# Image loads ahead of small weights, second-image statistics ahead of the last taps, and one attention step per convolution step in the last blocks

## Chip, cores and metric

The kernel runs on one core of a Trainium2 chip. The metric is the device time of one execution in microseconds (us); before the change it is 2064.95 us, the median of three runs from 2063.49 to 2067.5.

## What is computed

The input is two images of 256 channels and 56 x 56 pixels in float32. The first layer is a group norm, a 1x1 convolution to 768 channels, a 3x3 depthwise convolution, local attention in 7x7 windows (4 heads undilated, 4 heads at dilation 2), a projection and a residual:

```
x = x + _L0_conv_ref(_gn(x), w_qkv1, w_qkv2, rpb0, rpb1, w_proj)
t = _to_tokens(x)                                   # (2, 3136, 256)
t = t + _L1_attn_ref(_ln_t(t), Wq, Wk, Wv, Wm, W1, W2, g1, b1, g2, b2)
t = t + _L1_ffn_ref(_ln_t(t), Wr, br, ln_g, ln_b, W1, b1, W2, b2)
x = _from_tokens(t, x)
# in _gn:          (v - mean) / sqrt(var + eps), 32 groups of 8 channels
# in _L0_conv_ref: y = einsum(w_qkv1, x); y = depthwise 3x3 (y); 7x7 local attention; w_proj
# in _L1_attn_ref: Q, K = elu + 1; KV = sum K v; msg = Q KV Z; norm; two-layer feed-forward; norm
# in _L1_ffn_ref:  top 2 of 8 experts, 256 -> 1024 -> 256 with gelu
```

The second layer is linear attention with a feed-forward part, and a mixture of 8 experts with two experts per token.

## The kernel before

A planner of the programming framework puts the instructions of each engine into a queue. It works from the order in which the program emits them and from its own estimate of when inputs are ready; the program's order is the priority, and an instruction that is ready sooner may be put ahead of one that was emitted earlier. The kernel steers it with three means. `tc.issue_after(ins)` puts an instruction behind `ins` in the same engine's queue. `tc.high_priority()` raises the instructions inside it. `tc.manual_schedule` in `layer1` fixes TensorE's order to the order of emission. Once the queues are made, each engine takes its own in order.

**`front`** does layer 0 and the keys of the first half of layer 1's tokens. Its parts are generators, and the order in which they are advanced is the order of emission.

- `load_x(b)` (L399) loads one image into `x_sb`, in two halves of rows and two tiles of channels, each 784 KB: channel tile 0 from SP's queue, channel tile 1 from ACT's queue. For image 0 it is called at L412, after the loads of `g8` (the group-mean matrix) and `w2` (the depthwise weights, 27 KB in runs of 36 bytes) in ACT's queue (L407, L409). In the profile `x_sb` is named `t_a`, because the memory is used for tokens later.
- `norm_image` (L473) is the group norm. VectorE takes 14 `bn_stats` (L482) and two `bn_aggr` (L485); a matmul with `g8` (L488), a few VectorE operations and a second matmul (L494) give mean and variance of each group; POOL takes the power -0.5 (L143); VectorE then normalises `x_sb` in four pieces (L500). It yields twice inside the statistics and once after the power.
- `convolutions` (L505) goes over 2 images x 6 blocks `oc` of 128 output channels x 2 halves `hf` of the rows. POOL makes nine diagonal weight matrices per block (`diag`, L514, two blocks of buffers). For each half TensorE does the 1x1 convolution (L525, 16 matmuls), ScalarE copies it into a padded tile (L531), TensorE does the 3x3 taps of the first eight rows with the diagonals (L546, 18 matmuls), and VectorE the taps of the other 20 rows (L559, eight `scalar_tensor_tensor` after a first one on ScalarE, L557). SP stores the half to `yd` in memory (L566). In the last half of image 0, `(oc, hf) == (5, 1)`, it also issues `load_x(1)`, and the generator `behind = norm_image()` is advanced after taps 3, 5, 7 and after the store. In that half of image 1, ACT loads the tokens of the first half.
- `attend(b)` is the local attention of one image: `band0` and `band1` yield once per chunk of keys. A chunk (L580 on) is score matmuls (L589, 32 rows of the array per head), a bias and mask added by VectorE (L593), an exponential on ScalarE (L598), and the product with the values (L602, 32 columns per head). After each strip come accumulation (L609), a normalisation (L619 to L629) and the projection (L358, L363), stored to `td`. A band starts only when enough blocks of the convolution have been stored.
- The loop at L860 draws one step of `convolutions`, and then `advance(PACE[b])`: up to two steps of the attention, for either image. There are eight convolution steps in a block. When the convolutions end, `cv.close()` gives up their buffers, `tokens.open()` takes the memory for the keys, and 13 steps of `first_keys` alternate with `advance(3)`. `advance(10**6)` emits what is left of the attention.

**`layer1`** starts with `merged(0, ...)` (L1519 on), which folds the key sums of the first half into a matrix `mw`: transposes `kxt`, a product with `w_v` into PSUM (`kvt`, L1542), the head mask `m32` on VectorE (L1547), a product with `w_m` (L1551), and `centre(mw)`. Then 14 groups of tokens pass through queries, keys of the second half, messages, feed-forward and routing. After the first of these steps `prepare_feed_forward` calls `centre(fw2)` (L1478 to L1480 on VectorE). `newest[0]` is the last PSUM copy that the helper `evac` gave to VectorE.

The experts (L1380, L1398) follow until the end.

Of the kernel before, what the change touches and what calls it, by code (L numbers as in the profile page):

```python
# [14 lines left out]
ALU = mybir.AluOpType  # L15
# [4 lines left out]
P = 128  # L20
B, C, HH, WW = 2, 256, 56, 56
# [10 lines left out]
NEG = -1e30  # L32
KR = (8, 7)
KC = 14
PACE = (2, 2)

EDGE = (0, 4, 11, 18, 25, 28)
S1 = [-(-2 * WW * (EDGE[j + 1] - EDGE[j]) // 32) * 32 for j in range(5)]
# [80 lines left out]
def hybrid_kernel(ctx: ExitStack, tc: tile.TileContext, a: dict, out: bass.AP):  # L119
    nc = tc.nc  # L120
# [47 lines left out]
    newest = [None, None]  # L168
# [198 lines left out]
    def front(ph):  # L367
# [31 lines left out]
        def load_x(b):  # L399
            for hf in range(2):  # L400
                cols = slice(hf * T // 2, (hf + 1) * T // 2)
                for ct in range(2):
                    eng = nc.sync if ct == 0 else nc.scalar
                    eng.dma_start(x_sb[:, ct, cols], xv[b, :, ct, cols])

        g8 = cw.tile([P, P], F32, name="g8")
        nc.scalar.dma_start(g8, a["c_g8"])  # L407
        w2 = cw.tile([P, 6, 9], F32, name="w2")
        nc.scalar.dma_start(  # L409
            w2, a["L0_conv_w_qkv2"].rearrange("(oc p) one kh kw -> p oc (one kh kw)", p=P)  # L410
        )
        load_x(0)  # L412
        wq1 = cw.tile([P, 2, 3 * C], F32, name="wq1")
        nc.sync.dma_start(wq1, a["w_qkv1_t"].rearrange("(ct p) o -> p ct o", p=P))
        wpr = bp.tile([P, 2, C], F32, name="wpr")
# [57 lines left out]
        def norm_image():  # L473

            st = sp.tile([P, 2, NG, 6], F32, name="st")
            mv = sp.tile([P, 2, 2], F32, name="mv")
            for gs in (range(0, 3), range(3, NG)):
                for ct in range(2):  # L480
                    for g in gs:
                        nc.vector.bn_stats(st[:, ct, g, :], x_sb[:, ct, g * G : (g + 1) * G])  # L482
                yield
            for ct in range(2):
                nc.vector.bn_aggr(mv[:, ct, :], st[:, ct, :, :].rearrange("p g s -> p (g s)"))  # L485
            gps = ps_c.tile([P, 4], F32, name="gps", tag="pc")
            gm = sp.tile([P, 2], F32, name="gm")
            nc.tensor.matmul(gps[:, 0:2], g8, mv[:, :, 0], start=True, stop=True)  # L488
            nc.vector.tensor_copy(gm, gps[:, 0:2])
            dv = sp.tile([P, 2], F32, name="dv")  # L490
            nc.vector.tensor_tensor(dv, mv[:, :, 0], gm, ALU.subtract)
            nc.vector.tensor_tensor(dv, dv, dv, ALU.mult)
            nc.vector.tensor_tensor(dv, dv, mv[:, :, 1], ALU.add)
            nc.tensor.matmul(gps[:, 2:4], g8, dv, start=True, stop=True)  # L494
            grs, anchors["pow"] = rstd_of(sp, gps[:, 2:4], 1e-5, "gn")
            yield
            for hf in range(2):
                cols = slice(hf * T // 2, (hf + 1) * T // 2)
                for ct in range(2):
                    nc.vector.tensor_scalar(  # L500
                        x_sb[:, ct, cols], x_sb[:, ct, cols],
                        gm[:, ct : ct + 1], grs[:, ct : ct + 1], ALU.subtract, ALU.mult,
                    )

        def convolutions():  # L505


            for _ in norm_image():
                pass
            yield 0, 0  # L510
            for b, oc in ((b, oc) for b in range(B) for oc in range(6)):
                diag = yp.tile([P, 9, P], F32, name="diag")
                for tap in range(9):
                    nc.gpsimd.tensor_scalar(  # L514
                        diag[:, tap, :], ident, w2[:, oc, tap : tap + 1], 1.0, ALU.mult, ALU.mult
                    )
                for hf in range(2):

                    r0 = hf * HH // 2
                    ypad = ypads[hf]  # L520
                    q0 = r0 - hf
                    for g0, n in ((0, 8), (8, 8), (16, 8), (24, 5)):
                        py = ps_c.tile([P, 8, WW], F32, name="py", tag="pc")
                        for ct in range(2):
                            nc.tensor.matmul(  # L525
                                py[:, :n, :], wq1[:, ct, oc * P : (oc + 1) * P],
                                x_sb[:, ct, (q0 + g0) * WW : (q0 + g0 + n) * WW],
                                start=(ct == 0), stop=(ct == 1),
                            )
                        k0 = 1 - hf + g0  # L530
                        nc.scalar.copy(ypad[:, k0 : k0 + n, 1 : WW + 1], py[:, :n, :])  # L531
                    behind = iter(())
                    if (oc, hf) == (5, 1):

                        if b + 1 < B:
                            load_x(b + 1)
                            behind = norm_image()
                        else:
                            for n0 in range(0, NA, 4):
                                tokens.load(n0, min(4, NA - n0), nc.scalar)  # L540

                    yc = yp.tile([P, HH // 2, WW], F32, name="yc")
                    pc = ps_c.tile([P, 8, WW], F32, name="pc", tag="pc")
                    for tap in range(9):
                        dy, dx = divmod(tap, 3)
                        nc.tensor.matmul(  # L546
                            pc, diag[:, tap, :], ypad[:, dy : dy + 8, dx : dx + WW],
                            start=(tap == 0), stop=(tap == 8),
                        )
                    nc.scalar.copy(yc[:, 0:8, :], pc)  # L550
                    yield b, oc
                    for tap in range(9):
                        dy, dx = divmod(tap, 3)
                        src = ypad[:, 8 + dy : dy + HH // 2, dx : dx + WW]
                        w = w2[:, oc, tap : tap + 1]
                        if tap == 0:
                            nc.scalar.mul(yc[:, 8:, :], src, w)  # L557
                        else:
                            nc.vector.scalar_tensor_tensor(  # L559
                                yc[:, 8:, :], src, w, yc[:, 8:, :], ALU.mult, ALU.add  # L560
                            )
                        if tap in (3, 5, 7):
                            next(behind, None)
                        if tap % 3 == 2:
                            yield b, oc
                    st = nc.sync.dma_start(  # L566
                        yd[b][oc * P : (oc + 1) * P, hf * T // 2 : (hf + 1) * T // 2],
                        yc.rearrange("p h w -> p (h w)"),
                    )
                    anchors["store"] = st.ins  # L570
                    next(behind, None)
            yield B - 1, 6

        qT0 = bp.tile([P, HH, WW], F32, name="qT0")
# [56 lines left out]
        held = {}  # L631
# [215 lines left out]
        def advance(n):  # L847
            nonlocal at
            while n > 0 and at < B and need[at] <= done[at]:
                need[at] = next(atts[at], None)  # L850
                if need[at] is None:
                    at += 1
                n -= 1

        for k, (b, blocks_done) in enumerate(convolutions()):
            if k == 0:
                with tc.issue_after(anchors["pow"]):
                    bias_tables()
            done[b] = blocks_done
            if b > 0:  # L860
                done[b - 1] = 6
            advance(PACE[b])
        cv.close()
        ps_e = ph.enter_context(tc.tile_pool(name="p3pe", bufs=1, space=PSUM))
        tokens.open()
# [546 lines left out]
    def layer1(ctx, tk, behind=(None, None)):  # L1412
# [19 lines left out]
        with lin as ph:  # L1432
# [41 lines left out]
            def centre(w):  # L1474

                n = w.shape[1]
                m = sm.tile([P, 4], F32, name="wmean")
                nc.vector.tensor_reduce(m[:, :n], w, AX.X, ALU.add)  # L1478
                nc.vector.tensor_scalar(m[:, :n], m[:, :n], 1.0 / C, None, ALU.mult)
                nc.vector.tensor_tensor(w, w, m[:, :n].unsqueeze(2).to_broadcast([P, n, C]), ALU.subtract)  # L1480
# [1 line left out]
            hb = wp.tile([P, 4], F32, name="hb_sb")  # L1482

            def prepare_feed_forward():
                centre(fw2)

                hb_ps = ps_h.tile([P, 512], F32, name="hb", tag="h")
                for oc in range(4):
                    for k in range(2):
                        nc.tensor.matmul(  # L1490
                            hb_ps[:, oc : oc + 1], fw1[:, 2 + k, oc * P : (oc + 1) * P], g1b1[:, k, 1:2],
                            start=(k == 0), stop=(k == 1),
                        )
                nc.vector.tensor_copy(hb, hb_ps[:, 0:4])
                for k in range(2):
                    nc.vector.tensor_scalar(fw1[:, 2 + k, :], fw1[:, 2 + k, :], g1b1[:, k, 0:1], None, ALU.mult)
# [22 lines left out]
            def merged(b, kxs, kc):  # L1519
# [20 lines left out]
                for hg in range(2):  # L1540
                    for ct in range(2):
# [1 line left out]
                            pv[:, hg * P : (hg + 1) * P], w_v[:, ct, hg * P : (hg + 1) * P],  # L1543
                            kxt[:, ct, hg, :], start=(ct == 0), stop=(ct == 1),
                        )
                for hg in range(2):
                    nc.vector.tensor_tensor(kvt[:, hg, :], pv[:, hg * P : (hg + 1) * P], m32, ALU.mult)  # L1547
                yield
                pm = ps_a.tile([P, 512], F32, name="mwp", tag="a")
                for hg in range(2):  # L1550
# [450 lines left out]
```

## Time and profile before

| What | Value |
|---|---|
| median of 3 runs | 2064.95 us (2063.49 to 2067.5) |
| the profiled execution's own time | 2068.74 us |
| its span, first to last instruction | 2067.0 us |
| TensorE busy | 1930.8 us, 93% |
| VectorE busy | 1024.7 us, 50% |
| POOL, ScalarE busy | 670.4 us, 633.3 us |
| mean granted TensorE clock | 0.973 |
| first large matmul (L525) starts at | 27.34 us |
| image 1's first L525 starts at | 280.16 us |
| last L546 of the convolutions ends at | about 593 us |
| first keys (L275) on TensorE at | 626.67 us |
| last local-attention projection ends at | 793.5 us |
| experts from about | 1340 us to the end |

The times inside the kernel are positions in that one profiled execution, counted from its first instruction. In the lines quoted below, "PE" is TensorE, "DVE" is VectorE, "ACT" is ScalarE, "SPq" and "ACTq" are DMA issues by those engines, and `x4` is the number of instructions that a line merges. An arrow in brackets names what the engine waited for before it. In a table of windows, PEclk is the granted TensorE clock as a share of full speed.

### The profile page before, as it was taken

Reading aid. Unit: us, or ns where it says so; the run is one execution under the profiler, and the core shown is the slowest. Engines: PE = TensorE matmul, PEld = TensorE weight load, DVE = VectorE, ACT = ScalarE, POOL = GpSimd, SP = SyncE. Lnnn points to the kernel's source line nnn. Section 1 sums busy time; section 2 is a strip of 40 time slices with the busy share of each in tenths; the row PEclk is TensorE's granted clock in tenths of the full one; section 3 lists DMA queues with packets and bytes.
Section 4 is the critical chain, followed back from the end, with each engine's and each line's share of the span. In section 5 each row is a group of like instructions: output and inputs, shape, how many; then the busy total and the mean of one; then the engine's idle time right before and its main releaser. Section 6 shows DMA issues by size and latency. Waiting matters only on the chain.

```text
span 2067.0 us, 27940 instructions
## 1 busy us (share of the span) xinstructions
PE 1930.8 (93%) x10102; PEld 1353.2 (65%) x10102; DVE 1024.7 (50%) x2629; ACT 633.3 (31%) x1258; POOL 670.4 (32%) x772
## 2 busy tenths in 40 slices
PE   4999989999998888999999998999999999999996
PEld 2544444554435455566665657878888888888885
DVE  5978877775986656455555554342111211121111
ACT  1323323333333332334333333332222222222332
POOL 5621011111013333345534444543333323333221
PEclk9999989999979999999999999999999999999998
DMA  4642422335342115001111142567667676676995
GB/s 107 169 103 72 138 87 56 110 114 116 87 140 68 32 55 167 1 16 36 45 39 49 47 138 78 151 197 225 192 200 194 186 207 189 189 197 193 289 282 161
DMA packets 189785, 264.67 MB, mean 128 GB/s; under 512 B 26295, under 2 KB 149509, under 8 KB 189391
## 3 DMA queue, kind: packets, MB, share of 16 engines
q1 hardware_dynamic: 160782, 220.81, 34.9%
q0 software_dynamic: 20576, 29.75, 7.5%
q10 hardware_dynamic: 8272, 12.15, 1.8%
q8 instruction: 84, 1.38, 0.3%
q14 instruction: 71, 0.57, 0.1%
HBM read 196.38 MB, written 70.55 MB: 129 GB/s over the span
## 4 chain that ended last, share of the span: by engine, by line
PE 64%; DVE 14%; DMA 5%; POOL 4%; ACT 3%; issue 3%; SPq 1%; ACTq 0%; DVEq 0%; POOLq 0%
PE ph L1380 16%; PE py L1398 15%; PE p L1640 5%; PE po L602 4%; PE pc L546 4%; PE py L525 4%; DVE yc L559 3%; PE s_ps L589 3%; DVE p L593 2%; POOL rs L262 2%; DMA y<-yt,idi 2%; PE s_ps L363 2%; PE kp L293 2%; PE kx L306 2%; DMA xr<-xs 1%
## 5 line engine op out<-in xcount | busy, mean ns | idle before, releaser
L1380 PE MATMUL ph<-xe,w1e 128*128 128x256 f32 (+1 forms) x1696 | 362.3, 371 | 3.8 <-ACT hT L1384 2.3
L1398 PE MATMUL py<-w2e,hT 128*128 128x256 f32 x1616 | 359.0, 379 | 0.0
L1384 ACT ACTIVATE hT<-ph,sv 128x256 f32<-128x256 f32 (+1 forms) x424 | 196.4, 464 | 498.5 <-PE ph L1380 492.8
L1380 PEld LDWEIGHTS ph<-xe,w1e 128*128 128x128 f32 x1696 | 310.4, 191 | 45.7 <-ACT hT L1384 3.5
L1398 PEld LDWEIGHTS py<-w2e,hT 128*128 128x128 f32 x1616 | 302.5, 190 | 38.7
L559 DVE SCALAR_TENSOR_TENSOR yc<-ypad,w,yc 128x1120 f32<-128x1120 f32 x192 | 267.0, 1393 | 34.9 <-ACT yc L557 31.8
L160 POOL DMA_INDIRECT y<-yt,idi x101 | 161.2, 1596 | 225.6 <-DVE yt L1404 132.0
L546 PE MATMUL pc<-ypad,diag 128*128 128x448 f32 x432 | 174.4, 545 | 0.5 <-ACT ypad L531 0.5
L593 DVE TENSOR_TENSOR p<-s_ps,tab 98x340 f32<-98x340 f32 (+5 forms) x240 | 138.0, 601 | 62.4 <-PE s_ps L589 60.4
L598 ACT ACTIVATE p<-p 98x680 f32<-98x680 f32 (+5 forms) x120 | 111.8, 931 | 180.1 <-DVE p L593 175.3
L525 PE MATMUL py<-t_a,wq 128*128 128x448 f32 (+1 forms) x384 | 156.0, 536 | 9.1 <-DVE t_a L500 5.9
L1336 DVE CAST idi<-xr 128x2 int32<-128x2 f32 (+1 forms) x53 | 9.8, 185 | 305.8 <-DMA xr<-xs 301.0
L1404 DVE SCALAR_TENSOR_TENSOR yt<-py,eq,yt 128x256 f32<-128x256 f32 x101 | 48.6, 483 | 211.3 <-PE py L1398 209.7
L589 PE MATMUL s_ps<-qT,kT 32*98 32x170 f32 (+5 forms) x960 | 130.0, 410 | 20.7 <-DVE p L593 18.3
L262 POOL TENSOR_TENSOR rs<-rs,mhalf 128x2 f32<-128x2 f32 (+2 forms) x89 | 65.4, 741 | 197.0 <-DVE rs L261 155.5
L589 PEld LDWEIGHTS s_ps<-qT,kT 32*98 32x98 f32 (+1 forms) x960 | 57.2, 173 | 106.4 <-DVE p L593 61.1
L546 PEld LDWEIGHTS pc<-ypad,diag 128*128 128x128 f32 x432 | 78.1, 189 | 72.0 <-issue 68.4
L514 POOL TENSOR_SCALAR diag<-ident,w 128x128 f32<-128x128 f32 x108 | 77.6, 738 | 127.0 <-PE pc L546 118.0
L1362 POOL TENSOR_SCALAR yt<-b2e,eq 128x256 f32<-128x256 f32 x101 | 47.1, 475 | 213.1 <-DMA b2e<-in_L_ffn_b 213.0
L525 PEld LDWEIGHTS py<-t_a,wq 128*128 128x128 f32 x384 | 70.3, 196 | 70.1 <-issue 53.8
L160 POOL DMA_INDIRECT xs<-row,si x98 | 96.2, 981 | 57.8 <-DVE si L1764 30.5
L1640 PE MATMUL p<-m2T,fw 128*128 128x512 f32 (+2 forms) x224 | 93.8, 541 | 0.0
(357 smaller groups left out, 2585.5 us busy)
## 6 DMA issues: line engine op xcount, KB each, us to landing
w1e<-in_L_ffn_W SPq DMA_DIRECT2D x53, 1024.0 KB
w2e<-in_L_ffn_W SPq DMA_DIRECT2D x53, 1024.0 KB
yd<-yc SPq DMA_DIRECT2D x24, 784.0 KB
ld<-yd SPq DMA_DIRECT2D x28, 448.0 KB
xr<-xs SPq DMA_DIRECT2D x48, 260.0 KB
b2e<-in_L_ffn_b SPq DMA_DIRECT2D x53, 128.0 KB
yr<-y SPq DMA_DIRECT2D x11, 512.0 KB
td<-t_i SPq DMA_DIRECT2D x24, 224.0 KB
```

Source lines behind the costliest of these rows:

```text
L160: ins = nc.gpsimd.indirect_dma_start(out=dst[:, :], out_offset=bass.IndirectOffsetOnAxis(ap=index, axis=0), in_=src, in_offset=None, **kw,)
L262: newest[1] = nc.gpsimd.tensor_tensor(r[:, :n], r[:, :n], mhalf[:, :n], ALU.pow).ins
L525: nc.tensor.matmul(py[:, :n, :], wq1[:, ct, oc * P : (oc + 1) * P], x_sb[:, ct, (q0 + g0) * WW : (q0 + g0 + n) * WW], start=(ct == 0), sto ...
L546: nc.tensor.matmul(pc, diag[:, tap, :], ypad[:, dy : dy + 8, dx : dx + WW], start=(tap == 0), stop=(tap == 8),)
L559: nc.vector.scalar_tensor_tensor(yc[:, 8:, :], src, w, yc[:, 8:, :], ALU.mult, ALU.add)
L589: nc.tensor.matmul(s_ps[:nk, j, :n].rearrange("p (i j) -> p i j", j=nj), kT[hs], q[hs], start=True, stop=True,)
L593: nc.vector.tensor_tensor(p[:nk, 2 * pr : 2 * pr + 2, :n].rearrange("p h (i j) -> p h i j", j=nj), s_ps[:nk, :, :n].rearrange("p h (i j) - ...
L598: nc.scalar.activation(p[:nk, :, :n], p[:nk, :, :n], AF.Exp)
L1380: nc.tensor.matmul(p1, x.w1[:, ct, j * P : (j + 1) * P], x.xe[:, ct, :], start=(ct == 0), stop=(ct == 1),)
L1384: nc.scalar.activation(hT[:, j, :], p1, AF.Gelu, bias=x.sv[:, 4 + j : 5 + j])
L1398: nc.tensor.matmul(py, hT[:, j, h * P : (h + 1) * P], x.w2[:, j, :], start=(j == 0), stop=(j == NJ - 1),)
L1640: nc.tensor.matmul(p1[:, :w], fw1[:, k, oc * P : (oc + 1) * P], rhs, start=(k == 0), stop=(k == 3))
```

## The change

It has six parts.

1. `load_x(0)` stands ahead of the loads of `g8` and `w2`.
2. `norm_image` yields once after all statistics and aggregates instead of twice inside the statistics. The last aggregate is remembered as `anchors["stats"]`.
3. In the last half of image 0, the statistics of image 1 are emitted ahead of tap 4 (before: after taps 3 and 5), and tap 4 on VectorE is put behind the last aggregate. The group mean and the power follow after tap 4, and the normalisation after tap 5, both with high priority (before: after tap 7, and after the store).
4. `PACE` is 2 attention steps per convolution step while the block is below 5, and 1 from block 5 on, in both images.
5. `centre(fw2)` is put behind `newest[0]` on VectorE.
6. The two mask multiplications of `merged` get high priority.

```diff
-PACE = (2, 2)
+PACE = 2
...
+        load_x(0)
         g8 = cw.tile([P, P], F32, name="g8")
         nc.scalar.dma_start(g8, a["c_g8"])
         w2 = cw.tile([P, 6, 9], F32, name="w2")
...
-        load_x(0)
         wq1 = cw.tile([P, 2, 3 * C], F32, name="wq1")
...
             for gs in (range(0, 3), range(3, NG)):
                 for ct in range(2):
                     for g in gs:
                         nc.vector.bn_stats(st[:, ct, g, :], x_sb[:, ct, g * G : (g + 1) * G])
-                yield
             for ct in range(2):
-                nc.vector.bn_aggr(mv[:, ct, :], st[:, ct, :, :].rearrange("p g s -> p (g s)"))
+                anchors["stats"] = nc.vector.bn_aggr(
+                    mv[:, ct, :], st[:, ct, :, :].rearrange("p g s -> p (g s)")
+                ).ins
+            yield
...
+                        if tap == 4 and b + 1 < B:
+                            next(behind, None)
...
-                            nc.vector.scalar_tensor_tensor(
-                                yc[:, 8:, :], src, w, yc[:, 8:, :], ALU.mult, ALU.add
-                            )
-                        if tap in (3, 5, 7):
-                            next(behind, None)
+                            held = tap == 4 and b + 1 < B and (oc, hf) == (5, 1)
+                            with tc.issue_after(anchors["stats"]) if held else nullcontext():
+                                nc.vector.scalar_tensor_tensor(
+                                    yc[:, 8:, :], src, w, yc[:, 8:, :], ALU.mult, ALU.add
+                                )
+                        if tap in (4, 5):
+                            with tc.high_priority():
+                                next(behind, None)
...
                     anchors["store"] = st.ins
-                    next(behind, None)
...
-            advance(PACE[b])
+            advance(PACE if blocks_done < 5 else 1)
...
-                centre(fw2)
+                with tc.issue_after(newest[0]):
+                    centre(fw2)
...
-                for hg in range(2):
-                    nc.vector.tensor_tensor(kvt[:, hg, :], pv[:, hg * P : (hg + 1) * P], m32, ALU.mult)
+                with tc.high_priority():
+                    for hg in range(2):
+                        nc.vector.tensor_tensor(kvt[:, hg, :], pv[:, hg * P : (hg + 1) * P], m32, ALU.mult)
```

Counted from the generators, the convolution loop emits 131 of the 174 attention steps before the change and 122 after it: nine more are left for the time after the convolutions. Of those, 39 go with the keys in both kernels; after the last keys, 4 steps remain before and 13 after.

## The prediction

> **What bounds the kernel now.** I read the page first, then TensorE's waits stretch by stretch, then each engine's timeline around the places that the diff names, and the table of windows for the clock.
>
> ```profile
> PE 1930.8 (93%) x10102; PEld 1353.2 (65%) x10102; DVE 1024.7 (50%) x2629; ACT 633.3 (31%) x1258; POOL 670.4 (32%) x772
> PEclk9999989999979999999999999999999999999998
> ```
>
> TensorE is the bound: 93% busy, 136 us idle in all. A change of order can only win idle time, or time in which the clock was low. From 850 us on nothing in the diff differs (the experts alone are 727 us), so I look before that. The first place is the start:
>
> ```profile
> 5.84 1.68 DVE L482 BATCH_NORM_STATS2 st<-t_a 128x6 f32<-128x448 f32 x3 [4.84 <-DMA t_a<-in_x]
> 11.44 6.27 POOL L514 TENSOR_SCALAR diag<-ident,w 128x128 f32<-128x128 f32 x18 [8.95 <-DMA w<-in_L_conv_w_qkv]
> 12.93 3.78 DVE L482 BATCH_NORM_STATS2 st<-t_a 128x6 f32<-128x448 f32 x7 [5.41 <-DMA t_a<-in_x]
> 20.43 2.20 DVE L482 BATCH_NORM_STATS2 st<-t_a 128x6 f32<-128x448 f32 x4 [3.71 <-DMA t_a<-in_x]
> 25.43 0.72 POOL L143 TENSOR_TENSOR rs_gn<-rs_gn,mhalf 128x2 f32<-128x2 f32 x1 [6.94 <-DVE rs_gn L142]
> 27.34 8.15 PE L525 MATMUL py<-t_a,wq 128*128 128x448 f32 x16 [2.19 <-DVE t_a L500]
> ```
>
> The statistics wait three times for the image; the last piece is seen only at 20.43, and the first convolution starts 6.9 us later. The second place is the change of image:
>
> ```profile
> 257.31 2.72 DVE L482 BATCH_NORM_STATS2 st<-t_a 128x6 f32<-128x448 f32 x5
> 271.87 0.54 DVE L485 BATCH_NORM_AGGREGATE mv<-st 128x2 f32<-128x42 f32 x2
> 279.01 1.10 DVE L500 TENSOR_SCALAR t_a<-t_a,gm,rs_gn 128x1568 f32<-128x1568 f32 x1 [0.55 <-POOL rs_gn L143]
> 280.16 5.59 PE L525 MATMUL py<-t_a,wq 128*128 128x448 f32 x8 [3.70 <-DVE t_a L500]
> ```
>
> These statistics waited for no data: VectorE put attention and taps ahead of them. Meanwhile TensorE had attention alone. The windows (columns: length, then busy us of PE, PEld, DVE, ACT, POOL, then clock, DMA share, GB/s) show what that costs:
>
> ```profile
> 250.00:264.00 14.00, 12.39 (x107) 5.26 (x106) 13.82 (x24) 4.32 (x5) 3.99 (x10) 1.00 0.03 8
> 264.00:277.00 13.00, 12.06 (x98) 5.98 (x98) 9.84 (x21) 3.79 (x4) 0.00 (x0) 0.61 0.21 79
> 277.00:286.00 9.00, 5.84 (x10) 2.90 (x11) 7.36 (x10) 0.74 (x2) 0.73 (x1) 0.62 0.34 89
> 592.00:627.00 35.00, 30.54 (x238) 13.14 (x237) 27.58 (x70) 9.10 (x10) 9.80 (x13) 0.61 0.22 64
> 627.00:694.00 67.00, 57.38 (x446) 35.10 (x447) 47.02 (x114) 24.20 (x35) 22.38 (x27) 0.97 0.29 68
> ```
>
> Where attention runs alone (264 to 277, 592 to 627) the clock is 0.61; where convolutions or keys run with it, 0.97 to 1.00. Busy time there hides lost time. The third place is the mask of `merged`:
>
> ```profile
> 802.16 0.48 DVE L1547 TENSOR_TENSOR kvt_sb<-kvt,m 128x128 f32<-128x128 f32 x2
> 802.50 2.08 PE L1551 MATMUL mwp<-w_m,kvt_sb 128*128 128x256 f32 x4 [4.38 <-DVE kvt_sb L1547]
> ```
>
> [...] (16 L602 of one shape take 1.14 us at 258.6, 1.93 at 602.6)[...]. [...] ACT's queue had moved its last image bytes by 14.2 us, but the piece was seen at 20.43, just when SP's scattered 676-value load of the bias table (`turned`, issued 6.52) was done, 20.64. [...] Diagonals take 0.35 us alone (6.27/18) and 1.25 beside taps (22.45/18, at 66.9 us).
>
> **Part 1, image first.** Nothing is added; two ACT issues (0.40 + 0.47 us) and the 768 runs of 36 bytes of `w2` go behind the image. Image 0 is 3.21 MB; between 4 and 6 us the queues moved 421 GB/s. From 3.0 us it needs 7.6 us: 10.6. The first piece was seen about 0.9 us after its data, so the last at 11.5[...]. Eight statistics remain then: 8 x 0.54 = 4.3, end 15.8 (before: 22.6). From there to L525 was 4.7: 20.5 instead of 27.34, at best 6.8 us saved. What is late next is `w2`: its small runs start at 10.6 instead of 3.0, and took about 6.4 us by the DMA view of each us. POOL's 18 diagonals wait for it, and in POOL's queue they stood ahead of the power. I expect `w2` seen between 15.5 and[...] 21.5, and 0 to 18 diagonals (0 to 6.3 us) queued ahead of the power, whose free time is 18.7. L525 then starts between 20.5 and 29.7, that is -6.8 to +2.4. I take `w2` at 17 and nine diagonals (3.2): power 20.2, L525 22.1, **-5.2 us**. The bias tables later on POOL (to 66.8) keep their time; diagonals of block 2 follow until 78.2 and were wanted at 84.2, so 5.2 us still fit.
>
> **Parts 2 and 3, statistics of image 1.** The same 14 statistics and two aggregates (8.1 us of VectorE) move ahead of tap 4. The loads are not moved past anything: the second halves go out at 234.45 (SP) and 235.72 (ACT), right after the last L525 that reads the old image, and their data ran until about 242. Six statistics then left take 3.3: aggregate 246, not 271.87. From aggregate to L525 it took 4.8 us at the start, 8.3 here; so L525 of image 1 can come at 251 to 255, not 280. The added wait holds tap 4: behind it on VectorE are taps 5 to 8, attention adds (L593) and SP's store of the half. Before, tap 4 ran after 245 anyway, so it costs nothing if the planner's landing time is right; each us that it is early is a stalled VectorE (2.60 us at 219.1 before), starving L593. Worth is not 25 us, but what TensorE lost from 264 to 286: 22.0 - 17.9 = 4.1 idle and 13 x 0.39 + 9 x 0.38 = 8.5 of clock, 12.6. Lower end 0 (the stretch forms elsewhere), more only if the similar one at 310 to 326 (5.1 of clock) goes too. I take six tenths: **-7.5**.
>
> **Part 4, pace.** Nine steps leave the convolutions for after the last keys: about seven chunks. In 592.9 to 626.7, attention alone, ten chunks took 3.4 us each; in company one costs TensorE 2.4 (L589 1.25, L602 1.1). Seven lose 7 us; `merged` and the first queries can fill a part: +5.5, range 0 to 14 (4.4 each, as from 606 to 614.9). On the gain side the last half's taps crept from 576 to 606 with VectorE full; less attention ends them sooner and shortens the half-speed stretch before the keys (13.6 of clock + 4.5 idle): -3, range 0 to -8. Net **+2.5**.
>
> **Parts 5 and 6.** The masks could go at 798.1, when L1542 ends: L1551 3.6 us sooner. But VectorE is idle only 0.49 + 1.37 us between there and the `ks` (L245, 812.1) for which TensorE waits next, 2.53 us. So **-1.9**, range 0 to -3.6. `centre(fw2)` at 807.18 already followed the copy at 806.51; the new order costs 0. If it slipped ahead of L245 more than now, up to +2.
>
> **Sum:** -5.2 - 7.5 + 2.5 - 1.9 = -12.1. The profiled execution took 2068.74 (span 2067.0 and 1.7 around it), so 2056.6; it ran 3.8 above the median, so against the median 2064.95 - 12.1 = **2053**.
>
> **Rivals.** (a) *Power behind the diagonals*: part 1 gives nothing, the rest -6.9: 2058. For it: POOL's order before. Against: the power is emitted first. (b) *Given back*: TensorE is 93% full, and the attention-only stretch merely moves; only 2 us stay: 2063. For it: nine steps more run alone. (c) *Slower*: the tail after the last keys is attention alone at half clock, and image 1's last tokens, which wait for its projections, come late. Its price is 14 us; parts 1 to 3 pay 6 and the masks 2: 2071. It decides once the tail costs above 12. For it: 592 to 627. (d) *All of it*: 6.8 + 12.6 + 5.1 - 2.5 = 22: 2043.
>
> **Chances:** forecast 0.45 (own range 2047 to 2059), (a) 0.17, (b) 0.16, (c) 0.14, (d) 0.08. About 0.2% (4 us) is what a measurement can tell from no change. Faster: forecast, (d), most of (a), a little of (b): 0.67; same: the rest of (a), (b): 0.18; slower: 0.15. The range 2042 to 2068 leaves out (c) and a tail of (d).
>
> **What would show it.** First L525 near 22, power ahead of or among the diagonals; last L485 near 246 and image 1's L525 before 256; clock near 1.00 from 250 to 290; fewer than 35 us at 0.61 before the keys; L1551 without its wait. I am wrong if `w2` holds POOL, if VectorE idles on the second-half load, or if a low-clock stretch follows the last keys.

## The result, and the profile after

The changed kernel takes **2090.85 us** (median of 4 runs, 2087.42 to 2092.7) against 2065.72 for the kernel before (4 runs, 2063.49 to 2067.5): a ratio of 1.012, 95% interval 1.0102 to 1.0138. It is 25 us slower where 12 us faster was predicted. On a second chip the same kernel took 2086.14 against 2067.34 (1.0099, 1.0063 to 1.0136). The profiled execution took 2089.58 us, its span is 2087.8.

The page of the changed kernel, first the engines, then the row of the granted clock:

```profile
PE 1947.5 (93%) x10102; PEld 1364.5 (65%) x10102; DVE 1028.0 (49%) x2629; ACT 633.0 (30%) x1258; POOL 679.9 (33%) x772
PEclk9999999999978997999999999999999999999997
```

TensorE does the same 10102 matmuls and is busy 16.7 us longer, again at 93%. The row of the clock (slices of 52 us) now has three low slices in the first half: two from 574 to 678 us, and one from 783 to 835. The start of the changed kernel (line numbers differ from those before by up to eight: L482 is L481 here, L525 is L526, L589 is L595, L1551 is L1559):

```profile
10.97 4.32 DVE L481 BATCH_NORM_STATS2 st<-t_a 128x6 f32<-128x448 f32 x8 [0.55 <-DMA t_a<-in_x]
19.40 6.30 POOL L515 TENSOR_SCALAR diag<-ident,w 128x128 f32<-128x128 f32 x18 [16.90 <-DMA w<-in_L_conv_w_qkv]
25.64 0.85 POOL L726 MEMSET acc<- 128x896 f32 x1
26.45 0.73 POOL L143 TENSOR_TENSOR rs_gn<-rs_gn,mhalf 128x2 f32<-128x2 f32 x1
28.36 4.00 PE L526 MATMUL py<-t_a,wq 128*128 128x448 f32 x5 [10.56 <-DVE t_a L501]
```

The statistics end at 15.3 instead of 22.6 and the power's input is ready at 18.0, but the power runs at 26.45: POOL, idle for 16.90 us until `w2` is seen at 19.40, takes all 18 diagonals and a clear first, which stand ahead of the power in its queue. The first convolution is 1 us later than before. The change of image:

```profile
239.13 1.68 DVE L481 BATCH_NORM_STATS2 st<-t_a 128x6 f32<-128x448 f32 x3 [0.95 <-DMA t_a<-in_x]
254.46 0.53 DVE L483 BATCH_NORM_AGGREGATE mv<-st 128x2 f32<-128x42 f32 x2
260.36 1.86 POOL L143 TENSOR_TENSOR rs_gn<-rs_gn,mhalf 128x2 f32<-128x2 f32 x1 [1.34 <-DVE rs_gn L142]
263.41 7.96 PE L526 MATMUL py<-t_a,wq 128*128 128x448 f32 x16 [0.83 <-DVE t_a L501]
```

Image 1 starts 16.8 us sooner (263.41, not 280.16), and its last L547 comes 29.7 us sooner. The attention does not: most of its chunks are 4 to 8 us later through image 1's convolutions, and 20 us later at the end. The windows show where the clock was low (length, then busy us of PE, PEld, DVE, ACT, POOL, then clock, DMA share, GB/s):

```profile
250.00:264.00 14.00, 9.92 (x67) 4.67 (x66) 13.37 (x25) 2.42 (x3) 8.54 (x11) 0.76 0.02 5
264.00:277.00 13.00, 13.00 (x45) 6.21 (x44) 9.45 (x11) 4.08 (x6) 0.00 (x0) 0.86 0.51 154
562.00:604.70 42.70, 35.55 (x260) 17.27 (x258) 36.68 (x69) 13.22 (x19) 8.80 (x12) 0.76 0.46 133
770.00:797.00 27.00, 25.23 (x218) 13.46 (x219) 14.63 (x36) 6.98 (x10) 2.04 (x4) 0.62 0.11 33
797.00:815.00 18.00, 16.56 (x82) 10.93 (x82) 8.99 (x24) 3.22 (x7) 0.71 (x2) 0.91 0.53 151
```

The fourth row is new. After the last keys, 770 to 797, nine chunks of attention run alone at a clock of 0.62. Before, the same place (the 18 us after the last keys) was this:

```profile
628.00:776.00 148.00, 127.95 (x1007) 80.16 (x1008) 89.54 (x213) 48.06 (x70) 50.64 (x60) 0.97 0.21 53
776.00:794.00 18.00, 17.71 (x101) 12.35 (x99) 9.53 (x22) 2.29 (x5) 2.24 (x4) 1.00 0.44 120
```

Those were projections and queries at full clock. And the masks of `merged` in the changed kernel:

```profile
821.24 0.47 DVE L1555 TENSOR_TENSOR kvt_sb<-kvt,m 128x128 f32<-128x128 f32 x2
821.57 1.65 PE L1559 MATMUL mwp<-w_m,kvt_sb 128*128 128x256 f32 x3 [4.88 <-DVE kvt_sb L1555]
```

`kvt` is ready at 816.7, yet the masks come last in a row of statistics on VectorE; the wait is 4.9 us, not shorter than 4.4.

**A ledger.** From each trace I took, up to the first feed-forward matmul of layer 1 (L1640 before), TensorE's idle time and its busy time, and counted busy time at half clock as half. In both traces the granted clock is either 1.00 or 0.50 (in windows of 1 us it was 0.50 from 599 to 626 before, and from 777 to 800 in the changed kernel); half clock stands for the 0.50. In the changed kernel eight L293 took 1.99 us at 1.00 (at 639.03) and 3.78 at 0.50 (at 629.03). What is left is the work. It is the same in both kernels, 722.7 and 724.9 us; idle is 91.3 and 95.5, and time at half clock 85.3 and 105.8. So the 17.3 us that are lost up to there are 4 of idle, 10.9 of clock and 2 of work, which is as close as the method is. The runs say the same: each lists its span and mean clock, and span x (1 - clock) is the time lost to the clock. Over the 31 runs of before beside e1 it averages 56.7 us with 2007.3 left; over the 4 of the changed kernel 72.6 with 2016.1. Of the 25 us, 16 are clock; the runs don't tell idle time and work apart in the other 9.

The same by stage, for the kernels below (length in us, chunks of attention in it, us at half clock, of which half is lost; "alone" is from the last L546 to the first keys, counted as the first L293; the keys end at their last L293):

| kernel | convolutions | alone | keys | after the keys | sum |
|---|---|---|---|---|---|
| before | 592.3, 82, 34 | 35.7, 10, 27 | 148.4, 27, 10 | 76.1, 1, 14 | 852.6 |
| changed | 562.7, 76, 17 | 42.0, 8, 21 | 165.1, 27, 31 | 100.1, 9, 38 | 869.9 |
| pace alone (e1) | 566.2, 76, 34 | 39.3, 8, 17 | 160.8, 27, 21 | 99.7, 9, 38 | 866.0 |
| changed, four per key (e4) | 571.9, 76, 44 | 39.3, 8, 17 | 183.5, 36, 31 | 70.8, 0, 21 | 865.4 |
| pace, image 0 (e5) | 572.1, 76, 44 | 39.4, 8, 17 | 180.8, 35, 51 | 71.9, 1, 7 | 864.3 |
| pace, image 1 (e6) | 589.2, 82, 24 | 22.4, 6, 15 | 145.7, 23, 23 | 99.6, 9, 38 | 857.1 |
| large matmuls in the tail (e12) | 565.1, 76, 17 | 42.1, 8, 21 | 171.8, 27, 51 | 102.9, 9, 17 | 881.8 |
| attention ahead (e16) | 596.0, 82, 38 | 19.9, 4, 10 | 184.3, 33, 58 | 73.7, 1, 14 | 873.9 |
| three steps (e17) | 587.9, 82, 34 | 35.4, 10, 27 | 151.3, 28, 0 | 59.8, 0, 7 | 834.5 |

The work up to there is 721 to 728 us in all of them but e12, which adds 14. Single executions scatter: up to the keys, the changed kernel, e4 and e12 have one and the same order on TensorE, and 17, 44 and 17 us at half clock in the convolutions; up to the last keys the changed kernel and e12 have the same order too, and 31 and 51 us at half clock among the keys.

### The profile page after: what moved, and what is told of

The parts are those of the page before. It is cut to its first block, busy times and chain, and to the rows that moved or that the text cites. A ratio compares the mean times of both kernels' runs of the same rounds, so it can differ in the third digit from the quotient of the medians.

```text
span 2087.8 us, 27949 instructions
## 1 busy us (share of the span) xinstructions
PE 1947.5 (93%) x10102; PEld 1364.5 (65%) x10102; DVE 1028.0 (49%) x2629; ACT 633.0 (30%) x1258; POOL 679.9 (33%) x772
## 4 chain that ended last, share of the span: by engine, by line
PE 63%; DVE 16%; POOL 5%; DMA 4%; ACT 4%; issue 3%; SPq 0%; DVEq 0%; ACTq 0%; POOLq 0%
PE ph L1386 16%; PE py L1404 16%; PE p L1648 5%; DVE yc L565 5%; PE po L608 4%; PE py L526 4%; PE pc L547 3%; PE s_ps L595 3%; DVE p L599 2%; PE kp L293 2%; POOL rs L262 2%; DMA y<-yt,idi 2%; PE kx L306 2%; PE s_ps L363 1%; PE py L1660 1%
## 5 line engine op out<-in xcount | busy, mean ns | idle before, releaser
L547 PE MATMUL pc<-ypad,diag 128*128 128x448 f32 x432 | 173.5, 544 | 0.6 <-ACT ypad L532 0.6
L526 PE MATMUL py<-t_a,wq 128*128 128x448 f32 (+1 forms) x384 | 154.2, 532 | 14.6 <-DVE t_a L501 11.4
L595 PE MATMUL s_ps<-qT,kT 32*98 32x170 f32 (+5 forms) x960 | 138.4, 415 | 28.1 <-DVE p L599 21.2
L515 POOL TENSOR_SCALAR diag<-ident,w 128x128 f32<-128x128 f32 x108 | 84.2, 800 | 173.9 <-PE pc L547 157.0
L595 PEld LDWEIGHTS s_ps<-qT,kT 32*98 32x98 f32 (+1 forms) x960 | 60.3, 175 | 115.9 <-DVE p L599 65.8
L547 PEld LDWEIGHTS pc<-ypad,diag 128*128 128x128 f32 x432 | 78.6, 189 | 71.9 <-issue 69.5
L526 PEld LDWEIGHTS py<-t_a,wq 128*128 128x128 f32 x384 | 69.7, 195 | 76.3 <-issue 53.0
```

The lines of the kernel that those rows point to most:

```text
L526: nc.tensor.matmul(py[:, :n, :], wq1[:, ct, oc * P : (oc + 1) * P], x_sb[:, ct, (q0 + g0) * WW : (q0 + g0 + n) * WW], start=(ct == 0), sto ...
L547: nc.tensor.matmul(pc, diag[:, tap, :], ypad[:, dy : dy + 8, dx : dx + WW], start=(tap == 0), stop=(tap == 8),)
L595: nc.tensor.matmul(s_ps[:nk, j, :n].rearrange("p (i j) -> p i j", j=nj), kT[hs], q[hs], start=True, stop=True,)
```

## The experiments

My theory after the comparison was rival (c), the pace; the rival to it was that the earlier start of image 1 (parts 2 and 3) takes the convolutions away from beside the attention.

**e1, the pace alone.**

```diff
-            advance(PACE[b])
+            advance(PACE[b] if blocks_done < 5 else 1)
```

> The kernel before with one edit: one attention step per convolution step in block 5 of both images, two elsewhere. Theory (pace): the nine steps that leave the convolutions run after the last keys with nothing beside them at half clock, and the last projections and all of layer 1 come that much later; then this kernel alone is 15 to 25 us slower than before, its last chunk near 790 to 800 instead of 777, with a half-clock stretch of over 15 us after the last keys. Rival (statistics): the loss comes from image 1's earlier start, which takes convolution work away from beside the attention; then this kernel is within 4 us of before.

2083.26 us, 1.0104 (1.0086 to 1.0122): 17.7 us slower. The last keys come at 766.3 and the last chunk at 793.8 (columns as above):

```profile
766.30:793.80 27.50, 26.06 (x223) 13.78 (x225) 14.63 (x36) 6.97 (x10) 2.04 (x4) 0.60 0.12 32
```

A half-clock stretch of 23.9 us begins between them and ends at 796.0. Part 4 carries most of the loss.

**e2, the changed kernel with the old pace** (`advance(PACE)`).

> The changed kernel with two attention steps per convolution step everywhere, all other parts kept. Theory (pace): the loss of 25 us goes, and what is left are the gains of the statistics and the masks: 2050 to 2066 us. Rival (statistics): it stays 10 us or more above before, 2076 or later, since image 1's convolutions still run ahead of the attention.

2064.55, 0.9995 (0.9979 to 1.0012). The loss is gone; no gain is left. Image 1 still starts early (267.09), so its early start is not what costs: the rival falls.

**e3, the statistics alone** (the diff of parts 2 and 3 on the kernel before).

> The kernel before with the statistics of image 1 ahead of tap 4 and the raised norm steps, nothing else. Theory (pace): image 1's first convolution comes near 263 instead of 280, the low clock between 264 and 286 shrinks, and the time falls by 2 to 10 us. Rival (statistics): slower by 8 us or more.

2061.32, 0.9989 (0.9971 to 1.0007): perhaps 2 us, not told from nothing. There is no loss here either, but against the rival this run says less than e2: image 1 starts at 273.89, and counted from the first convolution of its own execution that is only some 1.5 us sooner than before.

**e4, the tail beside the keys** (`advance(4)` for `advance(3)` in the changed kernel).

> The changed kernel with four attention steps per key step instead of three, so that the 13 steps left after the last keys go beside the keys (13 key steps, 13 more steps). Theory (pace): with no attention left alone the tail from the last keys to the last projection shortens from 45 us towards 20, and the time falls by 12 us or more, to 2079 or below. Rival (statistics): the attention is late whatever it stands beside, and the time stays within 5 us of the changed kernel.

2086.18, 1.0099 (1.0063 to 1.0136). A miss: no chunk is left after the last keys and the two last stages take 254.3 us instead of 265.2, but the median fell by less than 5 us, not by 12, and beside the second measurement of the changed kernel (1.0099) by nothing. The keys' stage grew from 165 to 184 us.

**e5 and e6, the pace in one image only.**

```diff
-            advance(PACE[b])
+            advance(1 if (b, blocks_done) == (0, 5) else 2)           # e5
+            advance(1 if b == 1 and blocks_done >= 5 else 2)          # e6
```

> The kernel before with one attention step per convolution step only in block 5 of image 0. Counted from the code, the eight steps that leave there come back in block 4 of image 1, where before attention had run out of finished rows, so again four steps are left after the last keys. Theory (tail): without a tail there is no loss: 2052 to 2066 us. Rival (any thinning of attention beside convolutions costs, for TensorE is the bound): half of the 18 us of the pace change, 2072 or more.

> The kernel before with one attention step per convolution step only in block 5 of image 1: 13 steps instead of four are left after the last keys. Theory (tail): the whole loss of the pace change is here, 2080 to 2088 us, with the last chunk 20 us or more after the last keys. Rival (any thinning costs): about half of it, 2071 to 2077.

e5: 2076.57, 1.004 (1.0022 to 1.0058), 8 us slower. e6: 2083.63, 1.0082 (1.0051 to 1.0113), 15 to 17 us slower; its profiled execution was the quickest of the four. So image 1's block carries the tail and most of the loss, but the theory of the tail alone falls: e5 has no tail and loses. The trace of e5 shows why. Image 1's convolutions start 11 us earlier, the attention is 10 us later, and what lags behind runs between the first and the second key step (the columns as above):

```profile
612.00:645.00 33.00, 31.82 (x209) 14.75 (x208) 18.60 (x44) 8.45 (x10) 4.97 (x6) 0.59 0.06 18
```

TensorE is 96% busy there, with attention but for some 4 us of matmuls of the key steps, at a clock of 0.59. So attention without company costs here too, and not only after the keys. The losses of e5 and e6 together are more than the 17.7 of e1: they do not add.

**e7 and e12, is it the company?** Extra matmuls that nobody reads, ahead of each pair of score matmuls in the chunks emitted after the last keys of the changed kernel:

```diff
+                if warm[0]:                                           # e7
+                    nc.tensor.matmul(s_ps[:, 0, 320:448], ident, ident, start=True, stop=True)
...
+                if warm[0]:                                           # e12
+                    for j in range(2):
+                        nc.tensor.matmul(s_ps[:, j, 288:512], ident, wpr[:, 0, 0:224], start=True, stop=True)
```

> The changed kernel with one more matmul of 128x128 (rows it writes are read by nobody) ahead of each pair of score matmuls of the chunks emitted after the last keys: 14 matmuls, about 0.15 us each, 2 us of added work. Theory (clock): attention alone is slow because its matmuls of 32 rows or 32 columns leave the array at half clock; large matmuls mixed in end the stretch of 24 us at half clock earlier and the time falls by 4 to 12 us, to 2079 to 2087. Rival (attention alone is slow for its own waits, the clock follows): no gain, 2089 to 2094.

> The changed kernel with two matmuls of 128x128 by 224 ahead of each pair of score matmuls of the chunks emitted after the last keys (28 in all, read by nobody), a fourth to a third of TensorE's time there. One look, for the clock alone. Theory (small matmuls: the share of 32-row and 32-column work sets the clock): the half-clock stretch after the last keys, 24 us, shrinks to under 10. Rival (it is not the share of large matmuls): it stays over 17.

e7, 2 us of large matmuls among 30: 2101.8 (1.014, 1.0101 to 1.018), no help, the half-clock time after the keys even 47.8 us. e12, 14 us among 30, is one execution, of 2098.7 us; its keys, which the edit does not touch, had 20 us more at half clock than those of the changed kernel, so its time says nothing of the tail. What counts is the window from its last keys to its last chunk:

```profile
779.00:809.00 30.00, 29.79 (x271) 17.98 (x273) 14.98 (x36) 6.98 (x10) 1.11 (x2) 1.00 0.10 30
```

The half clock is gone from the window (the 17 us in the table come later, from 830 on). The nine chunks, seven of them with added work of 14 us in all, take 30.0 us; without it they take 27.5. So here the low clock of attention alone (0.60 in e1) came with its small matmuls (32 rows or 32 columns of the array), and large matmuls beside it (1.00 in e12) were nearly free. Gaps are no explanation: e12 has fewer of them (TensorE idles 0.2 us of 30, in e1 1.4 of 27.5), but in the keys of e17 below TensorE idles 10% at full clock, and in e5 above 4% at 0.59. No run added as many small matmuls instead, so that it is their size rests on this one execution and on e5 and e17.

**e8, part 1 with the power put ahead of the diagonals**, on the kernel before.

```diff
+        load_x(0)
         g8 = cw.tile([P, P], F32, name="g8")
...
+                with tc.issue_after(anchors["pow"]):
                     for tap in range(9):
```

> The kernel before with the image's loads first, and with the 9 diagonals of each block made to follow the power of the statistics on GpSimd. Theory (part 1 failed because 18 diagonals stood ahead of the power once the small weights came late): the power runs near 18.5, the first convolution starts at 19.5 to 21.5 instead of 22.5 to 27, and the time falls by 3 to 6 us, to 2059 to 2063. Rival (given back): the start moves but the first attention chunk stays at its place near 105 and the time stays within 2 us of before.

2070.11 against 2068.67, 1.0011 (0.9998 to 1.0024). The rival holds:

```profile
18.25 0.72 POOL L143 TENSOR_TENSOR rs_gn<-rs_gn,mhalf 128x2 f32<-128x2 f32 x1 [14.98 <-DVE rs_gn L142]
20.16 7.42 PE L526 MATMUL py<-t_a,wq 128*128 128x448 f32 x16 [2.19 <-DVE t_a L500]
54.10 3.39 SPq L643 DMA_DIRECT2D tab<-fp  x4
57.60 1.68 SPq L567 DMA_DIRECT2D yd<-yc  x1
65.09 1.23 ACT L558 ACTIVATE yc<-ypad,w 128x1120 f32<-128x1120 f32 x1 [12.63 <-DMA yd<-yc]
66.79 5.55 PE L526 MATMUL py<-t_a,wq 128*128 128x448 f32 x8 [6.48 <-ACT yc L551]
```

The first convolution starts at 20.16, 7 us earlier, as the sum for part 1 had it at best. But a store of a half stands in SP's queue behind loads of the bias tables (L643), which come no sooner (54.10, and 49.81 before); ScalarE waits 12.6 us for the store's buffer, and TensorE 6.5 for ScalarE. The convolution at 66.79 starts no earlier than before (66.56): the gain is gone.

**e9, e10, e11, the other parts on the changed kernel**, all on one chip; e9 is the changed kernel itself, e10 has the old order of loads, e11 the old statistics.

> The changed kernel itself, as the ground for the two beside it on this chip: slower than before by 20 to 28 us.

> The changed kernel with the order of the first loads as before (the two small loads ahead of the image). Theory (in the changed kernel the late small weights put 18 diagonals and a clear ahead of the power, so the first convolution starts at 27.5 to 29 against 22.5 to 27 with the old order): the first convolution starts 1 to 6 us earlier and the time falls by 0 to 5 us. Rival (a start that comes earlier is given back at the diagonals of block 2): no difference over 2 us.

> The changed kernel with the statistics of image 1 as before (spread over taps 3, 5, 7 and the store). Theory (the statistics bring image 1's convolutions forward but not the sum of the work, so they are worth only the low clock around the change of image, 2 to 5 us with the old pace): 0 to 6 us slower than the changed kernel. Rival (with the thinner pace the statistics add to the attention that is left over): 3 to 8 us faster.

e9 2086.14 (1.0099, 1.0063 to 1.0136), 18.8 us slower where 20 to 28 were expected; e10 2081.16 (1.0072, 1.0044 to 1.01), e11 2092.24 (1.0129, 1.0093 to 1.0164). By the medians part 1 costs 5 us and parts 2 and 3 gain 6 in this surrounding; the intervals overlap. For part 1 the start is firmer: in seven executions with the new order the first L525 starts at 27.5 to 30.6, mean 28.7; in twelve with the old, 22.5 to 27.3, mean 24.9.

**e13 and e14, what is left.** e13 is the kernel before with parts 5 and 6; e14 is the changed kernel with the old pace and the old loads.

> The kernel before with parts 5 and 6 alone (masks raised, centre of the experts' weights after the newest statistics). Theory: they move at most 2 us, 2063 to 2067 where before is at 2066, and TensorE's wait for the masks stays near 4.4 us, for in the changed kernel it was still 4.9. Rival (they are the rest of the loss that pace, loads and statistics leave open): 3 to 8 us slower.

> The changed kernel with the old pace and the old order of loads: statistics, masks and centre are what is left. Theory (parts 2 and 3 gain 4 to 6, part 1 costs 3 to 5, part 4 costs 18): 3 to 7 us faster than before, the only combination of the change's parts below before. Rival (with the old pace nothing of them is seen): within 2 us of before.

e13: 2070.04 against 2068.67, 0.9998 (0.9985 to 1.001). The wait for the masks does fall, which I had not expected, to 1.93 us, but a later start of `kx` before it (a wait of 2.54 for ScalarE instead of 1.4) takes part of it, and nothing is seen in the time. e14: 2068.44, 0.9993 (0.9973 to 1.0013). A miss of mine: with the old pace nothing of the statistics is seen either.

**e15 and e16, attention with less of it alone.** e15 adds to e14 a first key step at high priority and four attention steps per key step; e16 puts the attention steps of image 1's block 5 at high priority in the kernel before (`with tc.high_priority() if b == 1 and blocks_done >= 5 else nullcontext():` around `advance`).

> The kernel of the run beside it (old pace, old loads) with the first key step at high priority and four attention steps per key step. Theory (attention alone between the last convolution and the first keys is half speed for want of large matmuls): keys start 10 us or more earlier, the stretch at half clock of 20 to 37 us before them shrinks, and the time falls by 3 to 10 us more. Rival (the attention left over only moves behind the keys): no gain, or slower.

> The kernel before with the attention steps of image 1's block 5 at high priority, so that fewer of them are left between the last convolution and the first keys. Theory (attention alone runs at half clock for want of large matmuls): 4 to 6 chunks instead of 10 stand alone there, the half-clock time from the last convolution to the first key step falls from 27 us to under 18, and the time falls by 3 to 8 us against before. Rival (the stretch alone is only pushed behind the keys, as with earlier keys): no gain, or slower by 5 us or more.

Both miss: 2093.53 (1.011, 1.0076 to 1.0143) and 2078.37 (1.0068, 1.0041 to 1.0095). The stretch ahead of the keys did shrink, to 4 chunks in both, but the half-clock time came back among the keys, 42 and 58 us: in e16 there are 42 us between the third and the fourth key step. Here attention that was put ahead of the keys pushed them apart, and stood alone between them.

**e17 and e18, the opposite of part 4.**

```diff
-            advance(PACE[b])
+            advance(3 if b == 1 and blocks_done >= 5 else PACE[b])
```

> The kernel before with three attention steps per convolution step in block 5 of image 1, the opposite of part 4. Counted from the code only three more steps fit (finished rows run out), so one step is left after the last keys instead of four, all of them projections. Theory (what counts is chunks without company): at most three chunks move, 0 to 4 us faster. Rival (thicker attention makes VectorE the bound of the convolutions): 3 us or more slower.

> The changed kernel with the old order of loads and with three attention steps per convolution step in block 5 of image 1 instead of one (two elsewhere): statistics, masks and centre beside the opposite of part 4. Theory (the parts add: three steps gain 9 us, statistics 0 to 4): 8 to 13 us faster than before. Rival (the gain of three steps hangs on one particular order, and another start of image 1 undoes it): within 4 us of before.

e17: **2054.87** against 2064.12, 0.9954 (0.9935 to 0.9972). e18: **2054.72** against 2066.59, 0.9952 (0.9935 to 0.9969). Both beat before and after; e17 gains 9 us where 0 to 4 were expected. In e17 nothing changes up to the first keys but for a start 4 us earlier; then (keys, and the 5 us after them):

```profile
623.00:775.00 152.00, 136.45 (x1069) 86.48 (x1070) 95.70 (x225) 49.42 (x72) 51.47 (x60) 1.00 0.23 59
775.00:780.00 5.00, 5.00 (x28) 3.72 (x27) 1.81 (x3) 1.17 (x3) 1.90 (x3) 1.00 0.76 243
```

Three more steps are emitted with the convolutions, so each key step has later attention beside it and three projections less are left over. The keys run wholly at full clock with 12 us more work in them (by the ledger), and the stage after them is 16 us shorter. At the first L1640 this trace is 18 us ahead of that of before, 12 of them idle time and 7 clock; over the runs beside each other, 6 of the 9 us are clock. e18 shows that this does not hang on one order; nothing is seen of a gain of the statistics on top of it.

## Why the prediction was wrong

**What bounds the kernel** held: work is nearly constant (2 us more), and time is won or lost in idle time and clock. The windows at 0.61 were read rightly, as attention alone.

**Part 1** (-5.2). The statistics ended at 15.3 (15.8 predicted), and `w2` was seen at 19.40, inside 15.5 to 21.5. The 21.5 was an estimate from one pair of times before (the last piece of the image seen at 20.43, `turned` done at 20.64). Here ACT's queue had moved all of `w2` by 14 us, 5.4 before it was seen, and SP, which waited for `turned`, went on at 21.61; what `w2` waited for in between is not shown. I took 17 and nine diagonals ahead of the power; there were 18 and a clear, so rival (a) was the true case, at the price of about +4 against the mean start of the old order. And even the full gain is given back (e8), at a queue that the sum had not followed: SP's, where stores stand behind table loads. I had only followed the tables on POOL.

**Parts 2 and 3** (-7.5). The statistics do come sooner and image 1 starts at 263 instead of 280, but not at 251 to 255, and the aggregate came at 254.5, not 246: from 239 on, VectorE took the statistics one by one between attention and taps. Nor is the earlier start mainly theirs. Counted from the first convolution of its own execution, image 1 starts at 252.8 before, at 251.4 and 246.0 with the statistics and the old pace (e3, e14), at 241.3 with the pace alone (e1) and at 235.1 in the changed kernel: the thinner attention of part 4 brought more of it. The worth is 0 to 6 us (e3, e14, e11).

**Part 4** (+2.5) is the step that failed: its mechanism was named, its size was wrong. I priced the tail at +5.5 (seven chunks at 3.4 alone less 2.4 in company) and put -3 beside it for taps that end sooner. Measured alone, part 4 costs 17.7. The price alone was nearly right: 27.5 us for nine chunks, 3.1 each. Wrong was the saving. Seven chunks at 2.4 and 3 more should have brought the last keys 20 us forward; in e1 they came 10.2 forward, of which 4 are an earlier start. Two terms are behind this.

The 2.4 in company was too much, because it adds groups of matmuls that overlap in the trace of before:

```profile
258.59 0.58 PE L602 MATMUL po<-p,v 98*32 98x221 f32 x8
258.99 0.56 PE L602 MATMUL po<-p,ones 98*32 98x221 f32 x8
259.48 0.63 PE L589 MATMUL s_ps<-qT,kT 32*98 32x221 f32 x8
```

The first two add up to 1.14 us, but the third starts 0.89 after the first. Counted once, a chunk at full clock takes TensorE 1.9 us (mean from 100 to 592 us: 0.98 for its L589, 0.89 for its L602), and (30.0 - 14) / 9 = 1.8 in e12. So each chunk in the tail costs 1.2 to 1.3 us more than in company, not 1.0, and there are eight more of them, not seven: about 10 us. The table has it as 24 us more at half clock after the keys, of which 12 are lost; this one does not scatter, for in all six traces with this tail (the changed kernel twice, e1, e6, e10, e11) there are 37.5 us at half clock there.

The -3 did not come. The half-clock time ahead of the keys did fall, from 27 to 17, but among the keys it rose from 10 to 21 (one execution each, and the order of the changed kernel alone gave 31 and 51 there). The convolutions are 26 us shorter in e1, but 16 of these come back before the last keys. By the ledger 12 of the 16 are work, scores, transposes and projections of attention that had stood beside the convolutions, and none is clock. In all, e1's trace is 13.4 us behind that of before at the first L1640, and 11.6 of these are clock.

**Parts 5 and 6** (-1.9): 0, as far as can be told (e13). In the changed kernel the masks were raised and still came behind a dozen instructions of statistics, at 821.24.

**Rivals.** (c) named the mechanism, the place and the sign. Its price of 14 for the tail is near the 12 that the table shows lost there, and low beside all of part 4 (17.7), and the 6 and 2 us that the other parts should have paid were not there: 2071 became 2091.

**Open.** Part 4 (17.7), part 1 (about 4) and parts 2, 3 (0 to -6) make 16 to 22. The two measurements of the changed kernel are 25 and 19 us above before, so up to some 9 us of the first are not laid to a part; the clock of a single execution varies that much (over the 31 runs of before beside e1 the time lost to it was 43 to 64 us). Taking part 4 alone out of the changed kernel (e2) wins back all of it, so part 4 may cost more beside the other parts than on its own; no run here settles that.

## What to carry to other kernels

When a kernel's bound engine runs at two speeds, as TensorE did here (clock 1.00 and 0.50), draw up its ledger as work, idle and low clock; if the work is constant, ask of a reordering what it does to idle time, and which small matmuls lose the large ones beside them. Price a piece of work by what it adds to the engine's time, not by the sum of instructions that overlap. A chunk of small matmuls was cheap here beside large ones (1.8 to 1.9 us, 3.1 alone), so a thinner pace near the end of the large work left a rest that cost more later (17.7 us in e1), and three steps instead of two gained 9 us; but raising the same steps' priority (e16) lost 14. Before moving a load forward, follow each queue to the next stage: in e8 a start 7 us earlier was all given back by 66.79, at a store that stood behind loads in SP's queue.

## What the hardware showed that I had not expected

With large matmuls of no use beside it the tail's clock was full, 1.00 where e1 had 0.60: 14 us of added work cost 2.5 us there (e12, one execution), while 2 us of it did nothing (e7, 47.8 us at half clock after the keys). A clock of 0.59 stood beside TensorE 96% busy (e5), and a clock of 1.00 beside 90% (e17), so here the busy share did not tell the clock. And one order of instructions gave 17 or 44 us at half clock in the convolutions in different executions, which is some 14 us of time; over the 31 runs of before beside e1, the time lost to the clock scatters as much as the span itself (standard deviations of 5.0 and 4.6 us).
